# A four-layer graph network on one core: the symmetry check of two batches beside the LSTM, another order of turns, and weight folding moved from the second pass to the first

## The chip, the cores and the metric

The kernel runs on one core of a Trainium2 chip. The metric is device time in microseconds (us) from the first to the last instruction of one execution with what lies around it; lower is better. A core has TensorE (PE) for matrix products, VectorE (DVE) and ScalarE (ACT) for elementwise work, GpSimd (POOL), and SyncE (SP), which here issues almost all DMA transfers. Each engine takes its own instructions in the order in which they were written into its queue.

## The reference

There are 32 batches of 512 nodes with 128 features, and a 0/1 adjacency of 512 x 512 for each batch. Four layers follow one another; each reads relu(layernorm(x)) and adds to x.

```python
h = relu(layernorm(x));  x = x + attention(h, adj)        # layer 0: softmax over neighbours
h = relu(layernorm(x));  x = x + gcn_lstm(h, adj)         # layer 1
h = relu(layernorm(x));  x = x + nodes_4_layers(h, adj)   # layer 2
h = relu(layernorm(x));  x = x + prelu_gcn(h, adj)        # layer 3
```

Layer 1 convolves the last 128 nodes of each batch, runs an LSTM of 128 steps over them with all 32 batches side by side, and multiplies the normalised adjacency sums of h by the LSTM's result. Layer 2 consists of four small layers: neighbour sums over adj and over its transpose, each with its own weights (`ws`, `wd`), a term of the node itself (`wn`), and then a common matrix `wu` and tanh. The inputs make every adjacency symmetric, with ones on the diagonal.

## The kernel before

The kernel relies on symmetry: the two neighbour sums of layer 2 become one, and the weights can be multiplied together beforehand (`fold`: `ws` and `wd` with their parts of `wu`, `wn` with its part). Since it relies on that, it also checks it on the chip. For each batch the squared adjacency is written to DRAM as bf16 (`das`, L1491, from POOL), read back transposed (`aT`, L1493, from SP), and compared with the adjacency on VectorE (L1496); the number of differences decides at the end whether a general version runs instead.

The work comes in three stages.

- `pass_1(b)`, for all 32 batches: layernorm, the keys, queries and values of layer 0, attention for the last 128 nodes, and the convolution that feeds the LSTM. Keys and values go to DRAM.
- `lstm()`: 128 steps. A step is 4 small products in 32-row tiles of TensorE (`f_z`, L1234), two activations, two cell operations on VectorE (L1266 and L1267), a third activation, the product L1278 and a 32 x 32 transpose (L1279) that gives the next step its input. Beside it runs `pass_2(b)`: attention for the other 384 nodes, also in 32-row tiles (`f_s` L1325, `f_po` L1334). For the first 22 batches (`EARLY`) and the two of `FIRST` (26 and 27) it also loads and squares the whole adjacency; the early ones form layer 1's neighbour sums already (`aggregate`, L1419, tile `f_pg`) and put them into DRAM. `fold` came after batches 4, 7, 10 and 13 of this pass, one of layer 2's four small layers each time.
- `rest(b, turn)`: layers 1 to 3, in the order `FIRST`, then 0 to 25, then 28 to 31. It needs the LSTM's result. Batches that are not early form their sums here. In layer 2 each small layer is a product with the folded weights (`f_py`, L1523), a split into two fp32r parts (L1402, L1403), the neighbour sum (`f_pa`, L1419), a scaling by the inverse norms (L1530), the node's own term (L1534) and a tanh (L1538). In all turns but the first two and the last two the transpositions go through DMA (`MOVED`).

The order is not written by hand. Every operation is given to a planner (`Plan`) with its engine, an assumed duration, a rank, what it reads and writes, and a `gap`, the assumed time to landing of a transfer. The planner plays the schedule through and then writes each engine's instructions in order of the planned starts. LSTM steps have the ranks 0 to 127 and go first. The ranks of `rest` start at `last` = 30,000, those of pass 2 at `spared` = 20,000; pass 2 of batches 28 to 31 is ranked within `rest`, and the first two turns of `rest` are brought forward to the LSTM. Filler that may not delay an LSTM step by more than 0.15 us in the plan (`patience`) stands between the steps; aggregates and the products of `fold` have 1.3 us.

`hold_back` (L603) adds a wait: a transfer on SP with a rank from 20,000 to below 30,000 waits for the LSTM step that the plan has just before it, so that it isn't issued ahead of the LSTM.

Buffers: a whole adjacency sits in one of two "a" buffers, squared ones in one of six "ar" buffers. A batch's "a" buffer becomes free once its comparison (L1496) has read it. The weights for `fold` are loaded into an "ar" buffer.

```python
das = plan.fixed(dram.tile([N, N], BF, tag=f"s{b}", name=f"f_das_{b}"))
POOL(R + 2, 1.4, lambda: nc.gpsimd.dma_start(das.t.rearrange("(t p) j -> p t j", p=P), f32(ar.t)), [ar], [das], gap=6.0)
aT = new("y", (P, NT, N), f"f_aT_{b}", BF)
plan.op({"SP": (3.0, lambda: nc.sync.dma_start_transpose(out=aT.t, in_=das.t))}, R + 2, [das], [aT], gap=4.0)
```

Of the kernel before, what the change touches and what calls it, by code (L numbers as in the profile page):

```python
# [13 lines left out]
P = 128  # L14
# [507 lines left out]
class Plan:  # L522
# [76 lines left out]
    def hold_back(self, tc, made, o, steps):  # L599

        while len(steps) > 1 and steps[1][0] + self.ACROSS["SP"] < o.start:
            steps.pop(0)
        if self.spared <= o.rank < self.last and steps[0][0] + self.ACROSS["SP"] < o.start:  # L603
            tc.add_manual_dep(made.ins, steps[0][1].name, mybir.DependencyInfo(
                mybir.DependencyClass.Sync, mybir.DependencyReason.DATA), reason="issued in step with the LSTM")

    def run(self, tc, queues):
# [152 lines left out]
        self.order = order  # L760
        order.sort(key=lambda o: (o.start, o.no))
        steps = []
        with tc.manual_schedule(engines=queues):
            for o in order:
                made = o.engines[o.engine][1]()
                if o.engine == "DVE" and o.rank < self.URGENT:
                    steps.append((o.end, made.ins))
                if o.engine == "SP" and steps:
                    self.hold_back(tc, made, o, steps)


def symmetric(ctx, tc, x, adj, weights, cols, rows, lstm_b, prelu_a, out, fail):
# [18 lines left out]
    MANY = 512 // (4 * B)  # L791
    LATE = 4
    FIRST = [B - LATE - 2 + k for k in range(2)]
    EARLY = range(22)
    FOLDS = (4, 7, 10, 13)
    MOVED = range(2, B - 2)
    TURN = 32
    T_STEP = 0.22
# [24 lines left out]
    def f32(ap):  # L823
        return ap.bitcast(FP)
# [5 lines left out]
    def new(tag, shape, name, dtype=FP):  # L830
        return plan.cell(sb, tag, shape, dtype, name)
# [64 lines left out]
    nc.vector.memset(ones, 1.0)  # L896
    neg_half = const.tile([P, 2, NT], FP, name="f_neg_half")
    nc.vector.memset(neg_half, -0.5)
    viol = const.tile([P, B, 2], FP, name="f_viol")
    rinv = const.tile([P, B, NT], FP, name="f_rinv")  # L900
    ln1 = const.tile([P, B, 2, NT], FP, name="f_ln1")
    seq = const.tile([P, T, B], FP, name="f_seq")
# [386 lines left out]
    def pass_2(b):  # L1289
# [51 lines left out]
                                                                    xc.t[:, t, :], OP.mult, OP.add), [po, ri], [(xc, t)])  # L1341
        if whole and not early:
            begun[b] = a, xc, ar, deg
        else:
            DMA(R + 5, 192, lambda: nc.sync.dma_start(dx.t, xc.t[:, :L, :]), [(xc, t) for t in range(L)], [dx], gap=STORED)
        mv = ln_stats(R, xc, range(L), f"r{b}")
# [21 lines left out]
    def squares(rank, b, a, name):  # L1368

        ar = new("ar", (P, NT, N), f"f_ar{name}_{b}", FR)  # L1370
        deg = new("dg", (P, NT), f"f_deg{name}_{b}")
        for t in range(NT):
            ACT(rank, 0.62, lambda t=t: nc.scalar.activation(ar.t[:, t, :], a.t[:, t, :], AF.Square,  # L1373
                                                             accum_out=deg.t[:, t : t + 1]), [(a, t)], [(ar, t), (deg, t)])
        return ar, deg

    def diagonal(rank, ar, op):
        def fn():
# [54 lines left out]
    def rest(b, turn, lw_after):  # L1433
        R = 30_000 + turn * 10
        dkq, dv, dl, dx = kept[b]
        if b in begun:
            a, xc, ar, deg = begun[b]
        else:
            a = new("a", (P, NT, N), f"f_a3_{b}")
            xc = new("x", (P, NT, P), f"f_x3_{b}")  # L1440
            DMA(R, 1024, lambda: nc.sync.dma_start(a.t, adj[b].rearrange("(t p) j -> p t j", p=P)), [], [a])
# [43 lines left out]
        moved = turn in MOVED  # L1485
        xn = ln_full(R, xc, f"c2{b}", moved)

        das = plan.fixed(dram.tile([N, N], BF, tag=f"s{b}", name=f"f_das_{b}"))  # L1490
        POOL(R + 2, 1.4, lambda: nc.gpsimd.dma_start(das.t.rearrange("(t p) j -> p t j", p=P), f32(ar.t)), [ar], [das], gap=6.0)  # L1491
        aT = new("y", (P, NT, N), f"f_aT_{b}", BF)
        plan.op({"SP": (3.0, lambda: nc.sync.dma_start_transpose(out=aT.t, in_=das.t))}, R + 2, [das], [aT], gap=4.0)  # L1493
        for k in range(2):
            def differ(k=k):
                nc.vector.scalar_tensor_tensor(junk, flat(a.t[:, 2 * k : 2 * k + 2, :]), 1.0, flat(aT.t[:, 2 * k : 2 * k + 2, :]),  # L1496
                                               OP.mult, OP.not_equal, accum_out=viol[:, b, k : k + 1])
            differ_ops.append(DVE(R + 2, 1.2, differ, [a, aT], []))
# [93 lines left out]
    def counted():  # L1592
# [8 lines left out]
        DVE(R, 0.9, exponentials, [], [bads], after=sum_ops)  # L1601

        def places():
            nc.vector.tensor_reduce(bad[:, 1:2], flat(viol), AX.X, OP.add)
# [11 lines left out]
    sum_ops, differ_ops, late = [], [], []  # L1616
    junk = const.tile([P, 2 * N], BF, name="f_junk")
    for b in range(B):
        pass_1(b)
    end = lstm()  # L1620
    for b in range(B):
        pass_2(b)
        if b in FOLDS:
            fold(FOLDS.index(b), 20_000 + b * 10)
    for k, b in enumerate(FIRST + [b for b in range(B) if b not in FIRST]):
        rest(b, k, end)
    counted()
    E = mybir.EngineType
# [85 lines left out]
```

## Time and profile before

| | |
|---|---|
| median of 3 runs | 1302.67 us (1300.12 to 1302.93) |
| the profiled execution | 1305.92 us, its span 1304.0 us |
| mean granted TensorE clock | 0.993 |
| busy: TensorE, VectorE, ScalarE, POOL | 1268.1, 990.3, 830.2, 389.8 us |
| first and last LSTM product (L1234) | 181.8 and 503.3 us |
| median step of the LSTM (L1279 to L1279) | 2.32 us |
| symmetry check: comparisons (L1496) | 64, 1222 ns each, from 524.7 to 1221.2 us |
| transposes (L1493) on SP | 32, 2251 ns median, from 519.7 to 1211.9 us |
| `fold`: transposes, products | 21 from 231.5 us on, the last products at 390.6 us |

Three stretches follow from the LSTM's times: pass 1 to 181.8 us, the LSTM with pass 2 to 503.5 us, and the rest. A line of the sums by stretch gives the stretch, its length, the busy time and number of records of PE, PEld (weight loads), DVE, ACT and POOL, the granted clock, the share of the DMA engines and GB/s. A line of the timeline gives start, duration, engine, source line, operation, tiles (out<-in), shape and count; a bracket at its end is the idle time of the engine before it and what ended that. A line of the chain of waits gives start, duration and what held the chain. A product of fp32 operands is two records on TensorE, one of fp32r operands (the aggregates) is one; "128*32" marks a 32-row tile.

### The profile page before, as it was taken

The numbers are of one execution on the slowest core, as the hardware profiler recorded it, in microseconds if no ns is written. First come the engines' busy times: TensorE is split into PE (matmuls) and PEld (weight loads), VectorE is DVE, ScalarE is ACT, GpSimd is POOL, SyncE is SP. The second block draws the span as 40 slices with busy tenths as digits, with TensorE's granted clock in tenths as the row PEclk, the third lists the DMA queues.
The fourth block names the chain that finished last, engine by engine and source line by source line (L and its number), as shares of the span: only waits on it lengthen the run. The fifth ranks groups of instructions, "written<-read, shape, count | busy, mean of one in ns | idle before, by whom it ended". The sixth has DMA issues, their size and how long they took to land.

```text
span 1304.0 us, 32965 instructions
## 1 busy us (share of the span) xinstructions
PE 1268.1 (97%) x12087; PEld 976.6 (75%) x12087; DVE 990.3 (76%) x3284; ACT 830.2 (64%) x2079; POOL 389.8 (30%) x733
## 2 busy tenths in 40 slices
PE   9999999998999999899999999999999999999997
PEld 6888876666766677677778787787777877877774
DVE  7989878877978787587667677676776787787754
ACT  5666667777777554577566676666766665675423
POOL 4654533222222133232213223132231322332000
PEclk9999999999999999899999999999999999999998
DMA  8888888887746655889476667666676366673311
GB/s 259 270 275 285 265 271 273 257 262 252 246 140 215 209 182 139 198 191 243 103 152 156 155 163 163 154 159 154 162 160 144 86 136 145 139 170 65 50 33 35
DMA packets 300699, 232.03 MB, mean 178 GB/s; under 512 B 140656, under 2 KB 246128, under 8 KB 300528
## 3 DMA queue, kind: packets, MB, share of 16 engines
q1 hardware_dynamic: 283632, 213.06, 58.4%
q0 software_dynamic: 16896, 16.78, 8.4%
q8 instruction: 97, 1.59, 0.5%
q14 instruction: 74, 0.61, 0.2%
HBM read 136.19 MB, written 62.13 MB: 152 GB/s over the span
## 4 chain that ended last, share of the span: by engine, by line
PE 85%; DVE 5%; DMA 3%; ACT 2%; issue 2%; POOL 1%; SPq 0%; ACTq 0%; DVEq 0%
PE f_pa L1419 17%; PE f_py L1523 14%; PE f_pa L1534 14%; PE f_pg L1419 8%; PE f_po L1334 5%; PE f_s L1325 5%; PE f_z L1234 4%; PE f_pk L1141 2%; PE f_pol L1184 2%; PE f_pv L1157 2%; PE f_p L1575 2%; PE f_sl L1174 2%; PE f_pl L1477 2%; PE f_pd L1209 2%; PE f_pq L1316 1%
## 5 line engine op out<-in xcount | busy, mean ns | idle before, releaser
L1419 PE MATMUL f_pa<-f_ar,f_y 128*128 128x512 f32 x1024 | 295.6, 426 | 0.7 <-ACT f_y L1402 0.7
L1419 PEld LDWEIGHTS f_pa<-f_ar,f_y 128*128 128x128 f32 x1024 | 189.4, 188 | 72.1 <-issue 37.3
L1523 PE MATMUL f_py<-f_wf,f_n 128*128 128x128 f32 x1280 | 175.0, 276 | 0.0
L1523 PEld LDWEIGHTS f_py<-f_wf,f_n 128*128 128x128 f32 x1280 | 165.4, 192 | 9.3 <-ACT f_n L1538 1.4
L1534 PE MATMUL f_pa<-f_n,f_wf 128*128 128x512 f32 x320 | 153.0, 593 | 0.3 <-DVE f_pa L1530 0.3
L1538 ACT ACTIVATE f_n<-f_pa,f_bcol 128x512 f32<-128x512 f32 x128 | 88.3, 690 | 93.5 <-PE f_pa L1534 93.4
L1373 ACT ACTIVATE f_ar<-f_a 128x512 fp32r<-128x512 f32 x216 | 133.6, 621 | 5.3 <-PE f_pg L1419 3.1
L1402 ACT CAST f_y<-f_py 128x512 fp32r<-128x512 f32 x128 | 74.7, 584 | 93.7 <-PE f_py L1523 88.4
L1491 POOL DMA_DIRECT2D f_das<-f_ar x32 | 27.8, 868 | 354.0 <-ACT f_ar L1373 284.5
L1334 PE MATMUL f_po<-f_v,f_e 128*32 128x129 f32 x3072 | 106.3, 274 | 6.0 <-issue 5.9
L1334 PEld LDWEIGHTS f_po<-f_v,f_e 128*32 128x32 f32 x3072 | 89.3, 110 | 20.4 <-issue 13.2
L1403 DVE TENSOR_TENSOR f_y<-f_py,f_y 128x512 fp32r<-128x512 f32 x128 | 87.4, 686 | 22.0 <-ACT f_y L1402 21.8
L1325 PE MATMUL f_s<-f_q,f_k 128*32 128x384 f32 x1024 | 100.6, 490 | 0.0
L1530 DVE TENSOR_TENSOR f_pa<-f_pa,f_inv 128x512 f32<-128x512 f32 x128 | 86.6, 693 | 16.5 <-PE f_pa L1419 16.1
L1234 PE MATMUL f_z<-f_w,f_seq 128*32 128x128 f32 x2040 | 85.1, 277 | 10.6 <-DVE f_seq L1279 4.2
L1534 PEld LDWEIGHTS f_pa<-f_n,f_wf 128*128 128x128 f32 x320 | 57.9, 190 | 47.1 <-issue 37.7
L1234 PEld LDWEIGHTS f_z<-f_w,f_seq 128*32 128x32 f32 x2040 | 55.4, 109 | 48.1 <-issue 11.4
L1496 DVE SCALAR_TENSOR_TENSOR f_junk<-f_a,f_aT 128x1024 bf16<-128x1024 f32 x64 | 78.1, 1221 | 7.1 <-DMA f_aT<-f_das 6.1
L1419 PE MATMUL f_pg<-f_ar,f_xp_d 128*128 128x512 f32 x256 | 75.3, 417 | 0.3 <-DVE f_xp_d L1411 0.2
L1523 PE MATMUL f_py<-f_wf,f_T_c 128*128 128x128 f32 x448 | 72.9, 275 | 0.0
L1328 ACT ACTIVATE f_e<-f_s 128x384 f32<-128x384 f32 x128 | 60.8, 484 | 17.7 <-PE f_s L1325 9.9
L1096 DVE COPY f_hl_d<-f_n 128x1024 uint16<-128x1024 uint16 x28 | 19.4, 694 | 68.8 <-ACT f_n L1538 68.8
(197 smaller groups left out, 2756.8 us busy)
## 6 DMA issues: line engine op xcount, KB each, us to landing
f_a<-in_adj_dram SPq DMA_DIRECT2D x30, 1024.0 KB
f_a<-in_adj_dram SPq DMA_DIRECT2D x96, 256.0 KB
f_das<-f_ar POOLq DMA_DIRECT2D x32, 512.0 KB, 4.8
f_dkq<-f_kh SPq DMA_DIRECT2D x32, 448.0 KB
f_dv<-f_v SPq DMA_DIRECT2D x32, 258.0 KB
f_v<-f_dv SPq DMA_DIRECT2D x32, 258.0 KB
f_x<-in_x_dram SPq DMA_DIRECT2D x32, 256.0 KB
f_al<-in_adj_dram SPq DMA_DIRECT2D x32, 256.0 KB
```

Source lines behind the costliest of these rows:

```text
L1234: nc.tensor.matmul(z.t[part, k, :, :], h, w[:, m : m + 4, part], start=False, stop=True, skip_group_check=True)
L1325: PE(R, t_mm(NR), lambda s=s, j=j: quarters(lambda p: nc.tensor.matmul(s.t[p], keys.t[:, j * P + p.start : j * P + p.stop], q.t, start=Tru ...
L1334: PE(R, t_mm(P), lambda t=t, j=j: quarters(lambda p: nc.tensor.matmul(po.t[p, t, :], es[j].t[:, t * P + p.start : t * P + p.stop], v.t[:, ...
L1373: ACT(rank, 0.62, lambda t=t: nc.scalar.activation(ar.t[:, t, :], a.t[:, t, :], AF.Square, accum_out=deg.t[:, t : t + 1]), [(a, t)], [(ar, ...
L1402: ACT(rank, t_act(N), lambda: nc.scalar.copy(parts.t[:, :, 0, :], src.t), [src], [(parts, 0)])
L1403: DVE(rank, t_dve(N), lambda: nc.vector.tensor_sub(parts.t[:, :, 1, :], src.t, f32(parts.t[:, :, 0, :])), [src, (parts, 0)], [(parts, 1)])
L1419: nc.tensor.matmul(pg.t, parts.t[:, j, k, :], ar.t[:, j, :], start=(k == 0 and j == 0), stop=(k == 1 and j == NT - 1))
L1496: nc.vector.scalar_tensor_tensor(junk, flat(a.t[:, 2 * k : 2 * k + 2, :]), 1.0, flat(aT.t[:, 2 * k : 2 * k + 2, :]), OP.mult, OP.not_equal ...
L1523: nc.tensor.matmul(py.t[:, j, :], nodes[n].t[:, bass.ts(j, P)], wf[:, W_F[i] + c, 0, :], start=False, stop=(c == nch - 1), skip_group_chec ...
L1530: before = DVE(R, t_dve(N), lambda pa=pa: nc.vector.tensor_mul(pa.t, pa.t, inv_row.t), [inv_row], [pa])
L1534: nc.tensor.matmul(pa.t, wf[:, W_F[i] + c, 1, :], nodes[n].t, start=False, stop=(c == nch - 1), skip_group_check=True)
L1538: ACT(R, 0.57, lambda pa=pa, n=n, i=i: nc.scalar.activation(n.t, pa.t, AF.Tanh, bias=bcol[:, i : i + 1]), [pa], [n])
```

## The change

There are four parts. The check of the two batches of `FIRST` moves into a function `turned_back`, and for them it is called in pass 2, in four pieces a batch instead of two; for all other batches it stays in `rest`. The order of turns becomes `FIRST`, then 22 and 23 (`NEXT`), then the others; `NEXT` load their adjacency in four pieces, and the plan takes 8.0 instead of 4.0 us for their transposed copies to land. `fold` goes to pass 1, after batches 16, 20, 24 and 28. And `hold_back` now looks at whether a transfer is planned before the LSTM's end, not at whether its rank is below 30,000. The other lines adapt the counters (`viol`). `OPENING` and `FOLDS` are empty, and their loops do nothing.

```diff
@@ hold_back
-        if self.spared <= o.rank < self.last and steps[0][0] + self.ACROSS["SP"] < o.start:
+        if self.spared <= o.rank and o.start < self.left_at and steps[0][0] + self.ACROSS["SP"] < o.start:
@@ run
+        self.left_at = max(o.end for o in order if o.rank < self.URGENT)
@@ symmetric
+    NEXT = [22, 23]
     EARLY = range(22)
-    FOLDS = (4, 7, 10, 13)
+    OPENING = ()
+    FOLDS_1 = {16: 0, 20: 1, 24: 2, 28: 3}
+    FOLDS = {}
...
-    viol = const.tile([P, B, 2], FP, name="f_viol")
+    viol = const.tile([P, 2 * B + 2 * len(FIRST)], FP, name="f_viol")
@@ pass_2
         if whole and not early:
             begun[b] = a, xc, ar, deg
+            turned_back(R + 5, b, a, ar, NT)
@@ a new function
+    def turned_back(rank, b, a, ar, pieces):
+        das = plan.fixed(dram.tile([N, N], BF, tag=f"s{b}", name=f"f_das_{b}"))
+        POOL(rank, 1.4, lambda: nc.gpsimd.dma_start(das.t.rearrange("(t p) j -> p t j", p=P), f32(ar.t)), [ar], [das], gap=6.0)
+        aT = new("y", (P, NT, N), f"f_aT_{b}", BF)
+        plan.op({"SP": (3.0, lambda: nc.sync.dma_start_transpose(out=aT.t, in_=das.t))}, rank, [das], [aT], gap=8.0 if b in NEXT else 4.0)
+        n = NT // pieces
+        for k in range(pieces):
+            at = differs[0]
+            differs[0] += 1
+
+            def differ(k=k, at=at):
+                nc.vector.scalar_tensor_tensor(junk[:, : n * N], flat(a.t[:, n * k : n * (k + 1), :]), 1.0, flat(aT.t[:, n * k : n * (k + 1), :]),
+                                               OP.mult, OP.not_equal, accum_out=viol[:, at : at + 1])
+            differ_ops.append(DVE(rank, 0.08 + 0.56 * n, differ, [a, aT], []))
@@ rest
-            DMA(R, 1024, lambda: nc.sync.dma_start(a.t, adj[b].rearrange("(t p) j -> p t j", p=P)), [], [a])
+            if b in NEXT:
+                for t in range(NT):
+                    DMA(R, 256, lambda t=t: nc.sync.dma_start(a.t[:, t, :], adj[b, t * P : (t + 1) * P, :]), [], [(a, t)], gap=LANDED)
+            else:
+                DMA(R, 1024, lambda: nc.sync.dma_start(a.t, adj[b].rearrange("(t p) j -> p t j", p=P)), [], [a])
...
-        das = plan.fixed(dram.tile([N, N], BF, tag=f"s{b}", name=f"f_das_{b}"))
-        POOL(R + 2, 1.4, lambda: nc.gpsimd.dma_start(das.t.rearrange("(t p) j -> p t j", p=P), f32(ar.t)), [ar], [das], gap=6.0)
-        aT = new("y", (P, NT, N), f"f_aT_{b}", BF)
-        plan.op({"SP": (3.0, lambda: nc.sync.dma_start_transpose(out=aT.t, in_=das.t))}, R + 2, [das], [aT], gap=4.0)
-        for k in range(2):
...
+        if b not in begun:
+            turned_back(R + 2, b, a, ar, 2)
@@ the calls
+    for i in OPENING:
+        fold(i, HEAD + 0.35 + i)
     for b in range(B):
         pass_1(b)
+        if b in FOLDS_1:
+            fold(FOLDS_1[b], 10_000 + b * 10)
     end = lstm()
     for b in range(B):
         pass_2(b)
         if b in FOLDS:
-            fold(FOLDS.index(b), 20_000 + b * 10)
-    for k, b in enumerate(FIRST + [b for b in range(B) if b not in FIRST]):
+            fold(FOLDS[b], 20_000 + b * 10)
+    for k, b in enumerate(FIRST + NEXT + [b for b in range(B) if b not in FIRST + NEXT]):
         rest(b, k, end)
```

More of the change, by code (lines that the diff above doesn't have):

```diff
@@ L1486, in rest @@
         xn = ln_full(R, xc, f"c2{b}", moved)
-        das = plan.fixed(dram.tile([N, N], BF, tag=f"s{b}", name=f"f_das_{b}"))
-        POOL(R + 2, 1.4, lambda: nc.gpsimd.dma_start(das.t.rearrange("(t p) j -> p t j", p=P), f32(ar.t)), [ar], [das], gap=6.0)
-        aT = new("y", (P, NT, N), f"f_aT_{b}", BF)
-        plan.op({"SP": (3.0, lambda: nc.sync.dma_start_transpose(out=aT.t, in_=das.t))}, R + 2, [das], [aT], gap=4.0)
-        for k in range(2):
[L1495 to L1498, printed above, removed]
+        if b not in begun:
+            turned_back(R + 2, b, a, ar, 2)
         turned_d = new("dt", (P, TURN), f"f_dT_{b}")
@@ L1603, in places @@
         def places():
-            nc.vector.tensor_reduce(bad[:, 1:2], flat(viol), AX.X, OP.add)
+            nc.vector.tensor_reduce(bad[:, 1:2], viol, AX.X, OP.add)
             nc.vector.tensor_add(bad[:, 0:1], bad[:, 0:1], bad[:, 1:2])
@@ L1614, in counted @@
         PE(R, 0.1, read, [], [], after=[said] + late)
-    sum_ops, differ_ops, late = [], [], []
+    sum_ops, differ_ops, late, differs = [], [], [], [0]
     junk = const.tile([P, 2 * N], BF, name="f_junk")
+    for i in OPENING:
+        fold(i, HEAD + 0.35 + i)
     for b in range(B):
         pass_1(b)
+        if b in FOLDS_1:
+            fold(FOLDS_1[b], 10_000 + b * 10)
     end = lstm()
```

## The prediction

> **What bounds the kernel now.** I read the page's busy shares and slices first, then the sums by stretch, the timeline around the stall they show, and last the chain, for what one matrix pass costs.
>
> ```profile
> PE 1268.1 (97%) x12087; PEld 976.6 (75%) x12087; DVE 990.3 (76%) x3284; ACT 830.2 (64%) x2079; POOL 389.8 (30%) x733
> ...
> PE   9999999998999999899999999999999999999997
> ...
> PEclk9999999999999999899999999999999999999998
> ```
>
> TensorE is full in almost every slice: no other engine comes near. But its busy time is modelled, so I price its records by their pitch instead. The chain and the timeline give it:
>
> ```profile
> 1096.58 2.75 PE f_pa L1419 x12
> ...
> 1180.13 3.44 PE f_pa L1534 x8
> ...
> 1237.43 4.46 PE f_py L1523 x40
> ```
>
> ```profile
> 467.51 0.64 PE L1234 MATMUL f_z<-f_w,f_seq 128*32 128x128 f32 x16
> 467.95 1.98 PE L1334 MATMUL f_po<-f_v,f_e 128*32 128x129 f32 x64
> 469.72 0.65 PE L1234 MATMUL f_z<-f_w,f_seq 128*32 128x128 f32 x16
> ...
> 489.84 2.15 PE L1325 MATMUL f_s<-f_q,f_k 128*32 128x384 f32 x24
> 491.77 0.65 PE L1234 MATMUL f_z<-f_w,f_seq 128*32 128x128 f32 x16
> ```
>
> A record of an aggregate (fp32r, 512 columns) costs 0.230 us, of f32 with 512 columns 0.430, of f32 with 128 columns 0.1115 (two records a product: 0.223). In 32-row tiles, from start to start: 0.44/16 = 0.0275 for z, 1.77/64 = 0.0277 for f_po, 1.93/24 = 0.080 for f_s and f_pq. Every record priced and summed by stretch, against the stretch:
>
> ```profile
> 100.00:181.80 81.80, 81.77 (x735) 68.54 (x732) 70.39 (x293) 51.46 (x107) 39.50 (x102) 1.00 0.85 273
> 181.80:503.50 321.70, 305.08 (x6393) 215.25 (x6385) 265.28 (x1101) 223.69 (x792) 83.33 (x162) 0.99 0.72 224
> ...
> 516.00:540.00 24.00, 18.62 (x93) 14.06 (x92) 14.87 (x41) 11.98 (x30) 5.59 (x10) 0.86 0.73 191
> 540.00:1280.00 740.00, 739.53 (x3987) 577.53 (x3986) 538.11 (x1396) 466.66 (x999) 197.65 (x306) 1.00 0.62 139
> ```
>
> Pass 1 (to 181.8): 169.4 us of work, 12.4 lost, 6.5 of it in the first 20 us and only 2.3 between 100 and 180. LSTM with pass 2 beside it (to 503.5): 279.5 of work, 42.2 lost. The rest: 779.9 of 800.5, 20.6 lost; of these 10.4 lie between 500 and 540, some 10 in the last 24 us, next to nothing between. So the time is a fixed sum of matrix work, 1229 us, plus 75 us of losses: a change that only moves work is paid by what it does to the losses. The 10.4 us have a cause that the timeline names:
>
> ```profile
> 519.66 1.87 SPq L1493 DMA_TRANSPOSE f_aT<-f_das  x1
> ...
> 524.69 1.22 DVE L1496 SCALAR_TENSOR_TENSOR f_junk<-f_a,f_aT 128x1024 bf16<-128x1024 f32 x1 [3.35 <-DMA f_aT<-f_das]
> ...
> 525.84 0.69 DVE L1530 TENSOR_TENSOR f_pa<-f_pa,f_inv 128x512 f32<-128x512 f32 x1
> 526.44 0.15 DVE L1076 SCALAR_TENSOR_TENSOR f_sh_c<-f_mv_c,f_rs_c 128x4 f32<-128x4 f32 x1
> ...
> 526.59 2.08 PE L1534 MATMUL f_pa<-f_hT_c,f_wf 128*128 128x512 f32 x2 [3.78 <-DVE f_sh_c L1076]
> ...
> 528.14 3.40 SPq L1441 DMA_DIRECT2D f_a<-in_adj_dram  x2
> ```
>
> The comparison of batch 26 (L1496) waits on VectorE for its transposed copy, and behind it stand the scaling (L1530) and batch 27's LayerNorm, on which TensorE waits 3.78 us. Then it runs at half speed: two records take 1.87 us to the next start instead of 0.86, four transposes 0.98 instead of 0.44, eight f_py records 1.87 instead of 0.89. That costs 2.5 us or more. At 528.14 only is the adjacency of turns 2 and 3 loaded, since batches 26 and 27 keep both "a" buffers until compared: in this stretch TensorE has two batches and nothing else.
>
> **What the Trainium skill says.** "TensorE: Matmul & The Clock Gate", "What's actually happening": after an idle window the array runs at half its clock until it has been busy for about as long. The trace agrees: clock 0.86 in 516 to 540, records doubled after 3.78 us idle, not after 0.92. "Perfetto Trace Analysis", "Identifying the Most-Contended Engine": matrix busy share is a bad measure of what is left. Here too: 305 us busy, 279 of work in the LSTM stretch. The same page, "DMA Instruction — HWDGE": the recorded time of a DMA instruction isn't its data movement. Here 1.87 us on SP, 5.0 us to landing. "DVE: scalar operands, raw-bit mode, write accounting and state across instructions", "Flops that outlive an instruction": VectorE's queue is one in-order queue, as L1530 behind L1496 shows.
>
> **The change part by part.** Its order on each engine comes from a planner, so I counted TensorE's instructions in the two built programs before the first z, up to the last z, and after it.
>
> Folding: 21 transposes (0.11), 29 products (0.223) and 4 single columns: 9.5 us of TensorE, 7 x (0.49 + 0.37) = 6.0 us of ScalarE, 2.1 MB of loads, all moved from the LSTM stretch to pass 1. In return 20 quarter products of f_po and 16 of f_s slip out of pass 1 (20/4 x 0.222 + 16/4 x 0.645 = 3.7 us). Pass 1: +5.8 us of matrix work where 2.3 are free but spread in crumbs; I charge it in full. The 2.1 MB are 7.7 us at that stretch's 273 GB/s, with 15% of 82 us = 12 us of the DMA engines free: nothing to +3 us, taken +0.5. ScalarE (63% busy) and VectorE (+1.8 us, 86% busy) have room; each weight load stands 7 us or more ahead of its first use, by the times of the neighbouring loads and transposes in the trace.
>
> LSTM stretch: -9.5 (folding), 13 products of f_po and 4 of f_s more (13 x 0.222 + 4 x 0.645 = +5.5: the 3.7 of pass 1 and 1.8 from behind the LSTM), and four aggregates more, 24 against 20, now those of batches 20, 21, 26 and 27 too: 4 x 8 x 0.230 = +7.4. Net +3.4 of work. Losses: cutting the timeline at the LSTM's 128 transposes (L1279), the 17 steps with folding last 2.63 us for 2.10 of work, the 75 plain ones 2.41 for 2.10, the 36 with aggregates 2.70 for 2.40. So a folding step loses 0.22 more than a plain one and an aggregate step nothing more: 17 x 0.22 = -3.8. Added on VectorE: eight comparisons of 512 columns, as an estimate half of L1496's 1.22 plus 0.08 to read the sum, 0.69 each. They stand in pairs before the cell operation of steps 108 to 111, which comes some 0.95 us after the transpose: a pair of 1.4 us holds a step by 0.4, taken +1.0 in all (0 to 3). Stretch: +0.6.
>
> The wait added on SP: 212 of its DMAs, against 170, now wait for an LSTM step, among them those of batches 28 to 31 and of turns 2 and 3; everything behind them on SP waits too. Batches 0 to 27 were held so already, and the list of waits from 181 to 505 names no DMA above 1 us: I cost it at nothing, up to +3. The moved check also puts two transposes (2 us of SP each), and two stores on POOL (0.84 each, POOL 26% busy), into steps 104 to 108.
>
> The rest: -7.4 (aggregates) - 1.8 (8 products of f_po) = -9.2 of work. The stall: the comparisons of 26 and 27 are gone from here and both "a" buffers are free by step 111, so batches 22 and 23 are loaded and squared beside the LSTM. After the last z the order now has the sums of 22 and 23 (3.7 us), then six f_pl groups (5.3 us), then four batches instead of two. What is late next is the LayerNorm of batch 26: f_pl, tanh 1.14, update 0.69, statistics 0.87 and 0.37, POOL 1.3, normalising 0.9, some 7 us as in the trace (510.07 to 517.34), of which about 5 are covered; and the comparison of batch 22, whose copy should land about when VectorE reaches it. I leave 5 of the 10.4 us: -5.4 (bounds -9 and 0). The end is unchanged, and so are its 10 us.
>
> Sum: 5.8 + 0.5 + 0.6 - 9.2 - 5.4 = -7.7 us, from a span of 1304.0 (with what lies around it 1305.92). The median of the runs shown is 3.3 below the profiled run; the difference carried over, 1302.67 - 7.7 = 1295.0.
>
> **The rivals.** *A new stall in the same place.* With the LayerNorm late and batch 22's comparison late by what batch 26's was, nothing of the 10.4 is won: 5.8 + 0.5 + 0.6 - 9.2 = -2.3, 1300.4. For: the copy of 22 starts only after its sums. Against: four batches are at hand.
> *More goes than I take.* The transition closes to 2 us and step 115, 5.33 us in the trace with TensorE idle for 2.27 under "issue", does not recur (-3): -7.7 - 3.4 - 3 = -14, 1288.6. Against: such gaps of "issue" are spread over the stretch.
> *Slower: the comparisons hold the LSTM.* They stand in VectorE's queue before the cell operation, and all of TensorE waits for the LSTM. The copy of 26 is issued after step 104 and used after 108 (4 steps, 9.4 us), that of 27 after half of 107 and used after 110 (7 us), against 5.0 to landing. If SP is late by over 4.4 and 2.0 us, as in its 4.81 us at 470.80, each costs what it cost at 524: 3.8 + 2.5 = 6.3. Both, with 3 us for the held loads: -7.7 + 12.6 + 3 = +7.9, 1310.6. With one alone it ends near no change.
>
> **How the numbers follow.** My forecast 0.52, the same stall 0.19 (half of it within 0.2%), more 0.14, slower mechanism 0.15 (a third of it, one late copy, within 0.2%). 0.2% (2.6 us) is about what a measurement of this kernel can tell from no change: 1300.1 to 1305.3. Faster 0.52 + 0.14 + 0.09 = 0.75, less 0.01 for the forecast's own edge: 0.74; the same 0.10 + 0.05 = 0.15; slower 0.11. The forecast's own range is 1290 to 1300; with the cases beside it until 2 in 10 are left, 1288 to 1304.
>
> **What would show it.** Right: first z near 188, last z near 510, 500 to 540 of before with no VectorE wait on f_aT above 1 us and clock near 1.0, half or less of the 10.4 lost after the last z; steps 108 to 111 below 3.5 us. Wrong: waits of L1394's comparisons inside the LSTM, first z beyond 191, or TensorE waiting for loads of batches 28 to 31.

## The result, and the profile after

The changed kernel took 1310.1 us (median of 16 runs, 1303.84 to 1314.63), the kernel before, beside it, 1303.38 us (16 runs, 1298.9 to 1307.68). The ratio is 1.0044, 95% interval 1.0028 to 1.0059: slower by some 5.7 us, where 7.7 us less were forecast. A second measurement gave 1.0052 (1.0030 to 1.0075).

The profiled execution took 1303.84 us, the fastest of its 16; a second profile of the same kernel took 1309.06 us. Both are used below. From the page of the first, with busy time and slices as for the kernel before:

```profile
PE 1262.0 (97%) x12086; PEld 970.8 (75%) x12086; DVE 984.8 (76%) x3292; ACT 830.1 (64%) x2079; POOL 396.7 (30%) x733
...
PE   9999999999998989899999999999999999999997
...
PEclk9999999999999999999999999999999999999999
```

TensorE's busy time fell by 6 us, and the clock's one 8 of before, in the 17th slice with the stall, is gone. On TensorE's own line the 17th slice stays at 8, and instead of the 10th the 13th and 15th (391 to 423 and 456 to 488 us, within the LSTM) are at 8 now; nothing on the page says why. The first and last LSTM product, from the instructions of tile `f_z`, show how long the LSTM takes:

```profile
L1238 PE MATMUL f_z<-f_w,f_seq x2040: 269/273/298, 186.0 to 515.0; 128*32 128x128 f32 x186
```

They stood at 181.8 and 503.3 us. The sums by stretch (columns as before):

```profile
186.00:515.00 329.00, 306.25 (x6473) 211.30 (x6468) 273.43 (x1142) 228.99 (x809) 100.94 (x181) 1.00 0.76 232
...
516.00:540.00 24.00, 20.36 (x121) 15.79 (x119) 20.56 (x79) 15.75 (x41) 9.18 (x13) 1.00 0.68 128
540.00:1280.00 740.00, 739.58 (x3991) 578.24 (x3992) 526.56 (x1358) 461.06 (x980) 189.24 (x292) 1.00 0.62 136
```

The clock in 516 to 540 is 1.00, not 0.86: the stall there has shrunk. In the 36 us behind the last z some 6.4 us are lost, where it was 9.7. No comparison waits for its copy there, and TensorE's longest wait is 1.71 us, for a LayerNorm (L1080, at 529.10), as the prediction had it. With every TensorE record priced as in the prediction, the three stretches compare as follows (us; "lost" is length less priced work; the LSTM runs from the first to the last z, its steps from transpose to transpose, L1279 before and L1283 after):

| | before | forecast | first profile after | second |
|---|---|---|---|---|
| pass 1: length, work, lost | 181.8, 169.4, 12.4 | 188.1 | 186.0, 175.4, 10.6 | 187.9, 175.4, 12.5 |
| LSTM: length, work, lost | 321.5, 279.4, 42.0 | 322.1 | 329.0, 282.6, 46.3 | 332.5, 282.6, 49.8 |
| rest: length, work, lost | 800.8, 779.9, 20.9 | 786.2 | 787.0, 770.7, 16.3 | 786.9, 770.7, 16.2 |
| steps 1 to 100 of the LSTM | 252.6 | | 257.5 | 260.3 |
| steps 101 to 114 | 34.0 | | 40.4 | 40.4 |

Pass 1 and the rest are where the forecast put them. The LSTM stretch isn't: its work rose by 3.2 as forecast (3.4), but its losses rose by 4.3 and 7.8 where they should have fallen by 2.8. Steps 1 to 100 hold no comparison, and folding has left them, yet they are longer by 4.9 and 7.7 us. Some 3 us of that is priced work, since other work of pass 2 has moved up into them. Their losses rose by some 2 and 5 us, and those of steps 101 to 114, where the comparisons stand, by some 4 in both profiles.

What do they wait for? The waits of SP's own queue between 185 and 500 us (us in total, times, longest), first of the kernel before, then of the changed one:

```profile
SPq L1311 <- DMA f_dgT<-f_x: 15.4, 8, 3.9
```

```profile
SPq L1315 <- DMA f_dgT<-f_x: 65.4, 17, 5.7
SPq L1315 <- DMA f_dx<-f_x: 13.8, 4, 4.5
```

L1315 loads a batch's x in pass 2 (L1311 before). It needs one of the seven "x" buffers, and the buffer that it gets still has to be read by the store of an early batch's sums (`f_dgT`, L1366). SP takes its instructions in order, so while this load waits for that store to land, everything behind it waits too. The list of all waits between 185 and 517 us names two new victims, and third the comparisons that the prediction feared:

```profile
DVE f_x L1069 <- DMA f_dx<-f_x: 11.0, 8, 2.8
...
ACT f_x L1072 <- DMA f_dx<-f_x: 9.7, 7, 3.3
...
DVE f_junk L1394 <- DMA f_aT<-f_das: 3.7, 2, 2.0
```

L1069 and L1072 normalise x in place; they may overwrite it only when the store of the attention's result (`f_dx`, L1350) has read it. Neither line was in the list of before. SP's timeline shows a whole cycle (start, duration, queue, line, operation, tiles):

```profile
334.93 0.38 SPq L1366 DMA_DIRECT2D f_dgT<-f_x  x1
340.38 0.38 SPq L1315 DMA_DIRECT2D f_x<-in_x_dram  x1
340.85 0.44 SPq L1318 DMA_DIRECT2D f_x<-f_dl  x1
341.38 0.39 SPq L1314 DMA_DIRECT2D f_v<-f_dv  x1
341.88 0.37 SPq L1304 DMA_DIRECT2D f_k<-f_dkq  x1
342.35 0.84 SPq L1307 DMA_DIRECT2D f_a<-in_adj_dram  x2
343.29 0.38 SPq L1350 DMA_DIRECT2D f_dx<-f_x  x1
```

After the store of dgT at 334.93, SP issues nothing for over 5 us. Then it works off what has piled up, and the store of dx comes seventh. The timeline of all engines shows what that does to the LSTM:

```profile
346.54 0.25 ACT L1264 ACTIVATE f_th<-f_z 128x96 f32<-128x96 f32 x1
...
348.77 0.35 DVE L1069 TENSOR_SCALAR f_x<-f_x,f_ln,f_rs 128x128 f32<-128x128 f32 x1 [2.22 <-DMA f_dx<-f_x]
...
348.83 0.49 ACT L1072 ACTIVATE f_x<-f_x,f_sh_c,f_rs 128x128 f32<-128x128 f32 x1 [1.96 <-DMA f_dx<-f_x]
...
349.03 0.22 DVE L1270 SCALAR_TENSOR_TENSOR f_cu<-f_th 128x64 f32<-128x64 f32 x1
```

The step's activation (L1264) is done at 346.8. Its cell operation (L1270) starts at 349.03, since the normalisation waits at the head of VectorE's queue until the store of 343.29 has landed. The DMA view of 300 to 350 us in 40 slices (tenths of the 16 engines' time) shows the same as gaps:

```profile
DMA  9999950999999311699999211989999107887997
```

The DMA engines, busy in most slices, run all but dry four times in 50 us. The Trainium skill says in "DMA: Bandwidth & Descriptors", "Anatomy of one DMA — SWDGE (gpsimd) path", that the DMA engines never wait for a semaphore; the issuing sequencer does, before it hands the transfer over. The trace agrees: SP issues nothing from 335.31 to 340.38 us, and the slices from 338.75 to 341.25 stand at 1 and 0.

### The profile page after: what moved, and what is told of

Its sections match the earlier page's. It is cut to its first block, busy times and chain, and to the rows that moved or that the text cites. A ratio compares the mean times of both kernels' runs of the same rounds, so it can differ in the third digit from the quotient of the medians.

```text
span 1302.0 us, 33017 instructions
## 1 busy us (share of the span) xinstructions
PE 1262.0 (97%) x12086; PEld 970.8 (75%) x12086; DVE 984.8 (76%) x3292; ACT 830.1 (64%) x2079; POOL 396.7 (30%) x733
## 4 chain that ended last, share of the span: by engine, by line
PE 80%; DVE 8%; DMA 5%; ACT 3%; POOL 2%; issue 1%; SPq 0%; ACTq 0%; POOLq 0%; DVEq 0%
PE f_pa L1440 18%; PE f_py L1537 15%; PE f_pa L1548 15%; PE f_pg L1440 7%; PE f_po L1338 3%; DMA f_dx<-f_x 3%; PE f_z L1238 3%; PE f_s L1329 2%; PE f_p L1589 2%; PE f_pk L1145 2%; PE f_pv L1161 2%; PE f_pol L1188 2%; PE f_sl L1178 2%; PE f_pl L1502 2%; PE f_pd L1213 2%
## 5 line engine op out<-in xcount | busy, mean ns | idle before, releaser
L1537 PEld LDWEIGHTS f_py<-f_wf,f_n 128*128 128x128 f32 x1280 | 164.8, 191 | 12.4 <-issue 3.8
L1385 POOL DMA_DIRECT2D f_das<-f_ar x32 | 26.9, 842 | 359.0 <-ACT f_ar L1378 308.2
L1329 PE MATMUL f_s<-f_q,f_k 128*32 128x384 f32 x1024 | 102.2, 486 | 1.7 <-issue 1.7
L1394 DVE SCALAR_TENSOR_TENSOR f_junk<-f_a,f_aT 128x1024 bf16<-128x1024 f32 (+1 forms) x68 | 78.6, 1156 | 4.9 <-DMA f_aT<-f_das 3.7
L1100 DVE COPY f_hl_d<-f_n 128x1024 uint16<-128x1024 uint16 x28 | 19.4, 694 | 74.4 <-ACT f_n L1552 74.4
```

What stands on the lines that cost most here:

```text
L1329: PE(R, t_mm(NR), lambda s=s, j=j: quarters(lambda p: nc.tensor.matmul(s.t[p], keys.t[:, j * P + p.start : j * P + p.stop], q.t, start=Tru ...
L1394: nc.vector.scalar_tensor_tensor(junk[:, : n * N], flat(a.t[:, n * k : n * (k + 1), :]), 1.0, flat(aT.t[:, n * k : n * (k + 1), :]), OP.mu ...
L1537: nc.tensor.matmul(py.t[:, j, :], nodes[n].t[:, bass.ts(j, P)], wf[:, W_F[i] + c, 0, :], start=False, stop=(c == nch - 1), skip_group_chec ...
```

## The experiments

From this came four theories. A: with folding gone from the LSTM stretch the plan lets pass 2 run ahead until it is held by its x buffers, and puts the x load right behind the store of dgT; the wait on SP makes dx late and, through VectorE and ScalarE, the LSTM. B, the prediction's slower rival: the comparisons of batches 26 and 27 hold steps 101 to 114. C: the wider `hold_back` makes SP late. D: folding in pass 1 costs more than it saves. Each ratio below is to the kernel before, measured beside the kernel in question.

**The changed kernel again.**

> The changed kernel once more, for a second profile and an interval. Theory A (with folding gone from the LSTM stretch, SP's load of x stands right behind the store of dgT and waits for its landing, so the store of dx and with it the in-place normalisation come late): wait of the x load on the dgT store near 65 us in 185 to 500, waits of the normalisation on dx near 20 us, LSTM stretch (first to last z) 327 to 330 us, ratio to before 1.003 to 1.006. Theory B (the comparisons of batches 26 and 27 hold steps 100 to 113): the same ratio, with the loss of the stretch in steps 100 to 113 and no more than 2 us of it before step 100.

Ratio 1.0052 (1.0030 to 1.0075), 61.7 us of waits of the x load on dgT, 17.9 us of the normalisation on dx; the stretch, at 332.5 us, is 2.5 above A's range. Of the 11.0 us by which it is longer than before, 7.7 lie in the first 100 steps, some 3 of them work and the others losses, which B can't explain. Steps 101 to 114 are longer by 6.4, some 4 of them losses, so B has its share.

**Folding back in pass 2, the rest of the change kept.**

```diff
-    FOLDS_1 = {16: 0, 20: 1, 24: 2, 28: 3}
-    FOLDS = {}
+    FOLDS_1 = {}
+    FOLDS = {4: 0, 7: 1, 10: 2, 13: 3}
```

> The changed kernel with folding after batches 4, 7, 10 and 13 of pass 2 again; check beside the LSTM, order of turns and held loads stay. Theory A: the wait of the x load on the dgT store falls to 25 us or less, waits of the normalisation on dx to below 5 us; first z near 182, LSTM stretch near 330 (9.5 us of folding are back in it, the 7 us of losses gone); ratio to before 0.996 to 1.001. Theory B: the comparisons still hold steps 100 to 113: ratio 1.002 to 1.006. Theory D (folding in pass 1 costs more than it gives there): first z falls by 4 us or more and the LSTM stretch rises by less than that.

Ratio 1.0006 (0.9994 to 1.0018). The wait of the x load on dgT fell to 19.8 us, that of the normalisation to 1.3, and the first 100 steps took 252.8 us as before: A's part is as A said. But the stretch was 332.5 us long, and its losses 50.2. What they have gained lies at the end: step 115 lasted 7.85 us. The timeline there:

```profile
478.74 0.69 DVE L1394 SCALAR_TENSOR_TENSOR f_junk<-f_a,f_aT 128x512 bf16<-128x512 f32 x1 [3.76 <-DMA f_aT<-f_das]
...
479.36 0.19 DVE L1282 SCALAR_TENSOR_TENSOR f_h<-f_th,f_tcn 128x32 f32<-128x32 f32 x1
...
479.85 0.65 PE L1238 MATMUL f_z<-f_w,f_seq 128*32 128x128 f32 x16 [3.50 <-DVE f_seq L1283]
```

This is B: a comparison waits 3.76 us for its copy, behind it stands the LSTM's operation L1282, and TensorE waits 3.50 us for the step. Step 115 also holds 1.45 us of idle time under "issue", and step 125 lasted 6.51 us, with TensorE idle for 2.69 under "issue"; the cause of these stays open. So A and B are both real mechanisms, and this kernel trades the one for the other. D's sign came true as well: the first z comes 4.2 and 6.1 us earlier, and the stretch is longer by 3.5 and 0. But this run can't tell a cost of the folding itself from the wait that comes with it; two runs below can.

**Folding in pass 1 alone, on the kernel before.**

```diff
+    FOLDS_1 = {16: 0, 20: 1, 24: 2, 28: 3}
-    FOLDS = (4, 7, 10, 13)
+    FOLDS = ()
```

> The kernel before with folding in pass 1 as its only change; check of batches 26 and 27, order of turns and held loads as before. Theory A: the wait of the x load on the dgT store is 45 us or more, the normalisation waits for dx 10 us or more in sum, the losses of the LSTM stretch rise by 4 us or more, and the stall at 516 to 540 stays: ratio 1.000 to 1.005. Theory B: neither comparisons nor held loads are there, so the losses stay at 42 us or fall: ratio 0.996 to 1.000.

Ratio 1.0082 (1.0062 to 1.0102), above both forecasts. SP's waits, without any of the change's other parts, are nearly those of the changed kernel; the first 100 steps take 260.1 us:

```profile
SPq L1311 <- DMA f_dgT<-f_x: 59.5, 17, 6.1
```

So the folding's new place alone brings the wait. A missed in part: the losses of the stretch rose by some 2 us, where it said 4 or more; those of the first 100 steps did rise by some 4.5, and those of steps 101 to 114, with no comparison in them, fell by 2. What A didn't foresee at all: the rest, with the stall at 516 to 540 still in it, lost 26.7 us where it lost 20.9. 5.3 of that lie between 600 and 620, with TensorE idle for 4.32 us behind a transposed copy of h that came late; that isn't followed further.

**The planner told of the landing.** The planner counts a buffer as free when the last operation on it has been issued; it is free when that has landed. The new rule says so for the "x" buffers, with the 5.0 us (`STORED`) that the plan already takes for other stores.

```diff
-                c.free_at = max(c.free_at, o.end)
+                c.free_at = max(c.free_at, o.end + (o.gap if o.engine == "SP" and c.tag == "x" else 0.0))
...
-            DMA(R + 5, 256, lambda: nc.sync.dma_start(dg.t, flat(gT.t)), [gT], [dg])
+            DMA(R + 5, 256, lambda: nc.sync.dma_start(dg.t, flat(gT.t)), [gT], [dg], gap=STORED)
```

> The changed kernel, with the planner counting an x buffer as free when the store of dgT has landed and not when it has been issued; all else as changed, nothing left out. Theory A: the wait of the x load on the dgT store falls below 25 us, waits of the normalisation on dx below 6 us, the LSTM stretch to 321 to 325 us, ratio to before 0.996 to 1.001. Theory B or C (comparisons, or the wider hold): stretch 327 to 330 as in the changed kernel, ratio 1.002 to 1.006, whatever SP's waits become.

Ratio 0.9931 (0.9912 to 0.9950), 1295.92 us. SP's list has no wait of the x load on dgT any more and the other list none on dx. The stretch is 317.5 us with 37.4 lost, the first 100 steps take 246.3 us. That is A, but the stretch is 3.5 us below A's own range and the ratio below its 0.996: the rule changes the plan of all engines, and some 2.5 us of work have left the stretch (280.1 for 282.6). Four loads of x are still issued 0.38 to 0.70 us after a store of dgT and don't wait for it, so they need other buffers than that store's.

**The same order of work, 28 loads moved on SP.** The new rule changes the plan of all engines, so it could win in another way. This run leaves PE's, DVE's, ACT's and POOL's instruction order as in the changed kernel. Only in SP's queue do loads of x with their loads of dl, planned within 5 us of a store of dgT, stand two to five places later (15 loads of x and 13 of dl; the expectation counted too few). Such a load takes the hold of its new place, if it has one.

```diff
+        for o in [o for o in order if o.engine == "SP"]:
+            if o.mark == "dg":
+                stored = o.end
+            if o.mark == "xc" and o.start < stored + 5.0:
+                late = min(stored + 5.0, min(n.start for n in o.next) - 0.4)
...
+                    o.start = late
+        order.sort(key=lambda o: (o.start, o.no))
```

> The changed kernel with the planner's order on all engines unchanged, but in SP's queue 13 loads of x (with their loads of dl) stand up to 5 us later, behind the store of dx and others that followed them; nothing left out. Theory A: the wait of the x load on the dgT store falls from 60 to 65 us to below 25, waits of the normalisation on dx to below 6 us, steps 0 to 99 of the LSTM last 246 to 252 us instead of 257 to 260, ratio to before 0.994 to 0.999. If the new rule won by its other order of work and not by this wait: steps 0 to 99 stay at 255 or more, ratio 1.002 to 1.007.

Ratio 0.9933 (0.9910 to 0.9956), 1296.49 us, just below A's range. The wait of the x load on dgT is down to 1.8 us, and the next entry of its line in SP's list of waits is dx:

```profile
SPq L1329 <- DMA f_dx<-f_x: 11.8, 4, 3.2
```

(L1329 is the x load; the lines stand 14 lower here.) No normalisation waits for dx, the first 100 steps take 246.7 us, and the LSTM stretch, with the same 282.6 us of work, loses 36.2 us for 46.3 and 49.8. The DMA slices of 300 to 350 us have no hole left:

```profile
DMA  9999546969988668598965898999767888895467
```

This shows A: with the same work in the same order on four engines, and the same seven buffers, the place of 28 loads in one queue decides 1.1% to 1.2% of the time. Pass 1, LSTM and rest last 186.9, 318.8 and 786.5 us, 11.8 us below the profile of before. B is in this run as well, once:

```profile
448.40 5.18 SPq L1401 DMA_TRANSPOSE f_aT<-f_das  x1
...
457.13 0.69 DVE L1408 SCALAR_TENSOR_TENSOR f_junk<-f_a,f_aT 128x512 bf16<-128x512 f32 x1 [5.17 <-DMA f_aT<-f_das]
```

Step 108 lasted 7.92 us, 5.6 above the median step of 2.32.

**The new rule on the kernel before.** The same two lines.

> The kernel before with the planner's new rule alone (an x buffer is free when the store of dgT has landed); nothing left out. Theory A: the rule takes away what the change brought, and before had little of it (15.4 us of waits of the x load on dgT, no wait of the normalisation on dx): ratio to before 0.996 to 1.000. Rival (the rule is a better plan whatever is folded where): it gains here what it gained on the changed kernel, ratio 0.985 to 0.991.

Ratio 0.9982 (0.9973 to 0.9992). The rule takes 0.2% from a kernel that had 15.4 us of these waits, and 1.1% to 1.2% from one that had 61.7 and 65.4. It isn't a better plan in itself: the LSTM stretch becomes 8.5 us shorter here, but most of that is work that moves to the rest, which becomes 3.0 us longer in this profile.

**The new rule and folding in pass 1, on the kernel before.**

> The kernel before with folding in pass 1 and with the new rule; check, order of turns and held loads as before. Theory A: what folding in pass 1 alone cost (1.008) was the wait, so the ratio falls to 0.990 to 0.999, the waits of the x load on dgT are gone. Theory D (folding in pass 1 costs by itself): ratio 1.001 to 1.008.

Ratio 0.9919 (0.9896 to 0.9942), from 1.0082 without the rule. D falls: with the new rule on both sides, folding in pass 1 gains 0.6% (0.9919 against 0.9982).

**The new rule, folding back in pass 2.** The two edits from above together.

> The changed kernel with the new rule and folding after batches 4, 7, 10 and 13 of pass 2. By the prediction's own terms the move of folding is worth 5.8 + 0.5 - 9.5 + 3.7 of work brought forward and -3.8 of losses, about -3.3 us: without it the ratio to before is 0.994 to 0.998. Theory D (folding in pass 1 costs what it saves, or more, once no wait follows from it): 0.989 to 0.993, first z 6 us earlier and the LSTM stretch longer by less.

Ratio 0.9964 (0.9953 to 0.9976), within the range that the prediction's own terms give. Moving the folding is worth 0.0033 here once the wait is out of the way, 4 us. That the sum fits is partly luck: the first z comes 6.6 us earlier than with folding in pass 1 (6.3 by the prediction), but the LSTM stretch loses 46.0 us for 37.4, more than twice the 3.8 of the prediction, and since it has some 6 us less work, folding included, it is only 2.2 us longer and the rest 10.0.

**The new rule, the check of 26 and 27 back in the rest.**

```diff
@@ pass_2
-            turned_back(R + 5, b, a, ar, NT)
@@ rest
-        if b not in begun:
-            turned_back(R + 2, b, a, ar, 2)
+        turned_back(R + 2, b, a, ar, 2)
```

> The changed kernel with the new rule, and the check of batches 26 and 27 in the rest again, in two pieces a batch as for all others; folding in pass 1, order of turns and held loads stay. Theory A: the check beside the LSTM costs 1 to 3 us there and saves some 5 us of stall behind it: a stall with a wait of the comparison on its copy is back after the last z, ratio to before 0.994 to 0.998 (the new rule with the check beside the LSTM had 0.993). Theory B: the comparisons are what costs: ratio 0.988 to 0.992, steps 100 to 113 near 34 us.

Ratio 1.0036 (1.0021 to 1.0051), worse than either theory said. The LSTM stretch became 9.3 us shorter (308.2 us, 28.1 lost) with the same work. Of this 4.9 lie in steps 101 to 114, where the comparisons stood, and 3.2 in steps 1 to 100, where two profiles of one kernel differ by 2.8. So the check costs some 5 to 9 us beside the LSTM, not the +1.0 of the prediction. But the rest became 21.6 us longer. Between 560 and 580 alone 14.6 us are lost; TensorE waits there for a transposed copy of h:

```profile
575.70 1.78 PEld L1535 LDWEIGHTS f_py<-f_wf,f_T_c 128*128 128x128 f32 x8 [5.62 <-issue]
575.73 2.05 PE L1535 MATMUL f_py<-f_wf,f_T_c 128*128 128x128 f32 x8 [5.35 <-DVE f_T_c L1100]
```

Of four comparisons on VectorE two stand right before that copy of h, L1100 (from 572.43), and two behind it. How much of the 5.35 us they cost, and how much the copy's own transfer, isn't separated. The stall isn't back in its old place, 520 to 540, where next to nothing is lost; it has moved on and grown. With the new order of turns the check beside the LSTM is worth 12 to 14 us (spans 1293.6 and 1305.7; ratios 0.0105 apart).

**The new rule, the old condition for holding loads.**

```diff
-        if self.spared <= o.rank and o.start < self.left_at and steps[0][0] + self.ACROSS["SP"] < o.start:
+        if self.spared <= o.rank < self.last and steps[0][0] + self.ACROSS["SP"] < o.start:
```

> The changed kernel with the new rule and with the old condition for held loads (rank below 30,000, so the loads of batches 28 to 31 and of turns 2 and 3 wait for no LSTM step). Theory A: within 0.15% of the new rule with the wider hold: ratio to before 0.991 to 0.995. Theory C (the wider hold makes SP late): ratio 0.987 to 0.991. The other way: loads issued too early take SP from the LSTM stretch, ratio above 0.996.

Ratio 0.9918 (0.9898 to 0.9938) against 0.9931 (0.9912 to 0.9950): not to be told apart. C isn't shown; with the new rule at least, the wider hold costs little if anything.

**More time for the copies of 26 and 27.** In the kernel with the new rule two transfers of the check came late, a diagonal product that waited for the store of the squares and a comparison that waited for the copy:

```profile
449.03 0.69 DVE L1401 TENSOR_TENSOR f_ar<-f_ar,f_ident 128x512 fp32r<-128x512 f32 x1 [2.23 <-DMA f_das<-f_ar]
...
458.45 0.69 DVE L1394 SCALAR_TENSOR_TENSOR f_junk<-f_a,f_aT 128x512 bf16<-128x512 f32 x1 [1.49 <-DMA f_aT<-f_das]
```

They are steps 105 and 108, of 4.21 and 3.82 us. So the plan gets more time for both, with the new rule and the old hold:

```diff
-        POOL(rank, 1.4, lambda: nc.gpsimd.dma_start(das.t.rearrange("(t p) j -> p t j", p=P), f32(ar.t)), [ar], [das], gap=6.0)
+        POOL(rank, 1.4, lambda: nc.gpsimd.dma_start(das.t.rearrange("(t p) j -> p t j", p=P), f32(ar.t)), [ar], [das], gap=9.0 if b in FIRST else 6.0)
...
-        plan.op({"SP": (3.0, lambda: nc.sync.dma_start_transpose(out=aT.t, in_=das.t))}, rank, [das], [aT], gap=8.0 if b in NEXT else 4.0)
+        plan.op({"SP": (3.0, lambda: nc.sync.dma_start_transpose(out=aT.t, in_=das.t))}, rank, [das], [aT], gap=8.0 if b in NEXT + FIRST else 4.0)
```

> The changed kernel with the new rule, the old condition for held loads, and for batches 26 and 27 more time in the plan: 9.0 instead of 6.0 us for the store of the squares to land, 8.0 instead of 4.0 for the transposed copy. Theory B (what is left of the check beside the LSTM is late transfers: a comparison waits 1.5 us for its copy, a diagonal product 2.2 us for the store): these waits fall below 0.5 us, steps 100 to 113 to 35 us or less, ratio to before 0.988 to 0.991. If not late transfers but the work itself holds the steps: 0.991 to 0.994 as without the slack.

Ratio 0.9895 (0.9869 to 0.9920), 1291.38 us: the fastest kernel here, below both. Both waits are gone from the list, steps 101 to 114 take 34.6 us, the stretch 310.8 us with 30.4 lost. Its page:

```profile
PE   9999999999999999999999999999999999999996
...
PEclk9999999999999999999999999999999999999998
```

Its interval overlaps that of the run with the old hold alone (0.9918), so the time of the slack by itself isn't shown, only that the waits went.

**The slack alone, on the changed kernel**, with the old rule and the wide hold.

> The changed kernel with the old rule and the wide hold, and only the more generous times for batches 26 and 27 (9.0 us for the store of the squares, 8.0 us for the transposed copy). Theory A: the wait of the x load on dgT stays at 50 us or more and steps 0 to 99 at 255 to 261 us; if late copies are a second, smaller loss beside it, the comparisons' waits fall below 0.5 us, steps 100 to 113 to 37 us or less, and the ratio to before is 1.001 to 1.004. If the comparisons were the main loss (theory B): ratio below 0.998.

Ratio 1.0057 (1.0038 to 1.0076): no gain. Steps 101 to 114 fell to 36.9 us as foreseen, one comparison still waits 1.7 us, and the first 100 steps and SP's wait stay what they were:

```profile
SPq L1315 <- DMA f_dgT<-f_x: 59.4, 17, 5.8
```

The expectation of 1.001 to 1.004 counted a saving in 14 steps as a saving in the whole; the stretch is 329.9 us long, within the two profiles of the changed kernel.

The ratios side by side ("new check and turns" includes the wider hold):

| | old rule | new rule |
|---|---|---|
| folding in pass 2, old check and turns | 1 (before) | 0.9982 |
| folding in pass 1, old check and turns | 1.0082 | 0.9919 |
| folding in pass 2, new check and turns | 1.0006 | 0.9964 |
| folding in pass 1, new check and turns | 1.0044, 1.0052 (the change) | 0.9931 |

Down the left column folding in pass 1 costs 0.4% to 0.8%, down the right it gains 0.3% to 0.6%.

## Why the prediction was wrong

- **Pass 1, +6.3.** Right: +4.2 and +6.1. The work rose by 6.0 for 5.8 (175.4 less 169.4).
- **The rest, -9.2 - 5.4 = -14.6.** Right: -13.8 and -13.9, work -9.2, losses -4.6 and -4.7. The losses fell by nearly what was forecast (5.4), and what is left of the stall is the late LayerNorm, as forecast.
- **The LSTM stretch, +0.6. This step failed:** +7.5 and +11.0. Its work term (+3.4) was right at +3.2. What failed is the term for losses, "17 x 0.22 = -3.8": in the first 100 steps, which held the folding, the losses rose by some 2 and 5 us instead. The term took the loss of a folding step, 0.22 us above a plain one, for something that goes with the folding, and left the plain steps as they were. But with the folding gone the plan puts the load of x where it waits: the folding's move alone took this wait from 15.4 to 59.5 us. The prediction has no term for it; the wait on SP that it put "at nothing" is that of the held transfers. The run with folding back shows the first 100 steps at 252.8 us, the change at 257.5 to 260.3, and with the 28 loads moved on SP they are at 246.7, 5.9 below before in spite of some 3 us more work. So the sign of the term was right, and its size too small: some 9 us of losses go once the wait is out of the way, and the wait costs 11 to 14 us in these 100 steps.
- **Where I looked.** I read which engine waited for what, and found no DMA above 1 us. I didn't read the waits of SP's own queue, where 15.4 us of this very wait already stood, nor what stood behind the x load in it. The chain of waits of the kernel before has one of them too (start, duration, what held it); the next load of x was issued 3.27 us after this store:

```profile
255.30 3.21 DMA f_dgT<-f_x
```

And of the change I counted TensorE's instructions by stretch; the order on SP, which the built programs also show, I checked only for holds. As SP issues them in the traces, the next x load stands by only one place behind a store of dgT for 8 of 20 batches in the changed kernel and for 3 before, by more than two places for 7 and for 10.

- **The comparisons, +1.0 (0 to 3).** Too low. The losses of steps 101 to 114 rose by some 4 us, and with the new rule the check costs some 5 to 9 us beside the LSTM. Steps 108 and 110 lasted 4.46 and 4.49 us in the first profile, forecast below 3.5, with waits of 1.7 and 2.0 us for a copy; in the second profile step 108 lasted 6.32. What the slower rival priced at 6.3 us for one late copy was 5.6 in step 108 of the run with moved loads. Its mechanism was right and its time, 1310.6, is near the result, yet it is the smaller part of what made the change slow: in the run with the slack alone, which takes 3.5 us of it away in steps 101 to 114, the ratio is 1.0057.
- **The held loads, 0 to +3.** Nothing measurable, with the new rule (0.9918 against 0.9931).
- **"More goes than I take."** Step 115 of before, 5.33 us, lasts 2.21 after. That much of this rival came true.
- **With the wait gone.** The run with the 28 loads moved stands at 0.9933, and the forecast at 0.9941 (1295.0 of 1302.67). Pass 1 is longer by 5.1 us (6.3 forecast) and the rest shorter by 14.3 (14.6), but the LSTM stretch is shorter by 2.7 where +0.6 was forecast: a saving that was priced too low and a late copy that was priced too low go opposite ways. So it is partly luck that the sum comes so near.
- **Profiled and measured time.** The two profiled times differ by -2.1 and +3.1 us from the profiled time of before. They stood 6.3 and 3.5 us below the medians measured with them, that of before 2.5 and 0.7 us above the medians of before, which gives +6.7 and +7.4, the differences of the medians.

The Trainium skill has a related pattern, in "Perfetto Trace Analysis", "Optimization Strategy": the same gap repeating over a stretch on the engine that should be saturated can mean that there isn't room to allocate the next tile. The trace agrees in part. The load of x waits 17 times for a buffer that is still being read, but the repeating gap is on SP and the DMA engines rather than on TensorE, and more room wasn't needed: with the same seven buffers the later place of the loads removed it. Whether an eighth buffer does as well wasn't tried, nor were stores from another engine's queue.

That the planner chose the early place because it takes a buffer as free at the issue of the store is shown as far as the new rule goes: told of the landing, it chose other places and the wait was gone. Why it chose later places while folding was in pass 2 is only argued: folding kept TensorE and an "ar" buffer busy, and so pass 2 wasn't yet held by its x buffers. The 3 us more of other work in steps 1 to 100 of the changed kernel fit this.

## What to carry to other kernels

The queue that issues all transfers was an in-order engine here like any other: before removing filler from a stretch, read the waits of that queue, and ask of its longest wait what stands behind it. A load into a reused buffer should not stand right behind the store that empties this buffer; two to five places later it waited for next to nothing here (1.8 us in all), and what stood behind it went out in time. A store of another buffer just before it did no harm. A planner should count a buffer as free when the transfer out of it has landed, not when it has been issued; this one otherwise put load and store together once the folding no longer kept them apart.

## What the runs showed that was not expected

- A store of 256 KB blocked the buffer's next load for 5.45 us after its issue (334.93 to 340.38), and the wait was up to 5.7 us long. As an estimate from "DMA: Bandwidth & Descriptors" of the Trainium skill, same section as above, 2.0 us and 256 KB at 436 GB/s make 2.6 us. That figure is for another issue path; here, with other transfers under way (the slices stand at 9 until 338.75 us), the trace has twice that.
- A late transposed copy behind which the LSTM stands cost it some 3.5 to 5.6 us: TensorE waited 3.50 us in the step of 7.85 us, and the steps of 6.32 and 7.92 us were 4.0 and 5.6 above the median.
- Some 60 to 65 us of waits on SP in steps 1 to 100 became 11 to 14 us of lost time on the path: most of the wait was covered.
